# The 12-bit upper halves: from a VectorE bit shift to a ScalarE copy that rounds

## The chip, the cores and the metric

The kernel runs on one core of one Trainium2 chip. The metric is the device time of one execution in microseconds (us). The engines are written as in the profile: PE (TensorE matmul) and PEld (its weight loads), DVE (VectorE), ACT (ScalarE), POOL (GpSimd) and SP (SyncE, which issues the DMAs).

## The reference

The input is `x` (32 batches, 64 channels, 1024 positions) and a condition of 128 numbers for each batch. Two layers follow each other, and each has two parts.

The first part is a style-modulated stack of four 1-D convolutions (same, upsample, same, downsample, each with a kernel of 3), in which every batch has weights of its own:

```python
s = style @ mw.T + mb
weight = SCALE * w * s[:, None, :, None]
demod = lax.rsqrt(jnp.sum(weight * weight, axis=(2, 3)) + EPS)
weight = weight * demod[:, :, None, None]
```

The second part is a feed-forward block over tokens of 1024 numbers. In layer 0 it takes the 16 best of 64 experts, each a pair of rank-16 matrices (`h = x A`, gates, `o = (h * gate) B`). In layer 1 it is a product with int4 weights that have scales, zeros and a bias. All of it is to be computed at float32 precision.

## The kernel before, in words

**Tiling.** The 32 batches are 16 pairs `p`; a pair fills the 128 partitions with 2 x 64 channels for the convolutions. In the feed-forward part the partitions hold tokens or features. The convolution weights of a pair are first composed into one chain (`f`, L619, and `g`, L596, on PE; ACT copies `f` at L634 to L637, POOL adds at L642 to L652). `first` computes `c` (three matmuls, L768 and L773), ACT makes `yt` (L770), DVE adds (L774) and takes differences (L716), of which POOL takes more (L722, L730). `rest` makes the products `r` (L834, L843, L875) and `p` (L826), DVE adds (L865, L866, L883) and mends the edges with COPY_PREDICATED (L884). That is done for each half `h` of a pair.

**Exact products from short halves.** PE multiplies fast in the type float32r, which holds fewer bits than float32. So a number is cut into an upper and a lower half of 12 bits. `split` (L913 to L923) does this for the tokens: `high` (L149) clears the lower 12 bits by two shifts on DVE, PSUM to SBUF; DVE subtracts the result from PSUM, which gives the lower half `tl` (L919); ACT casts the upper half to `th` (L923). In layer 1 the cast of the second half of a pair is kept in a list (`held`) and put out later by `let_go` (L913). `turned_h` (L1079) does the same with transposed `h`, in tiles `ht`. `split_weights` does it for the weights `wa` and `wb`: shift on DVE (L149), subtraction on POOL (L374), cast on ACT (L375), and a DVE operation for the crossed term (L382). `scaled_low` (ACT, L927) scales the lower half and `crossed` (POOL, L935) makes `td`. The products are `h` and `o` (both L955) in layer 0 and `q` (L1204) in layer 1. The pairs 0 and 1 use plain float32 in layer 0.

**Stages.** The loop of layer 0 does the convolutions of the pairs beside the first product of the feed-forward block; its steady step takes 21.69 us (L826 at 201.37 and 223.06). A middle loop turns the gated `h` and makes the second product `o`. The loop of layer 1 does the convolutions of a pair beside `q` of the pair before.

**Order.** Work is put out in an order written by hand (lists like `beside`, and `yield` inside `layer0` and `layer1`, which lets the other work in). A scheduler then orders each engine's instructions; `tc.issue_after(x)` tells it to place an instruction behind `x`. PSUM banks come from three pools: `cps` with 3 banks (`c`, `r` and `ht`), `mps` with 1, and `fps` with 4 (`f`, `q`, and layer 1's second `r`). A new tile in a pool waits for the last reader of the tile that held its bank.

**Weights of layer 1's evacuation.** In `layer1` three pieces `q` (c = 0, 1, 2) of 342 columns are scaled by DVE into `sc` (L1228), added to `o` by POOL (L1230), and a scalar term is added by DVE (L1226). A copy of one element on POOL (`turn`, L1215) marks when the scales of the next pair may be loaded.

Of the kernel before, what the change touches and what calls it, by code (L numbers as in the profile page):

```python
# [8 lines left out]
F32 = mybir.dt.float32  # L9
I32 = mybir.dt.int32  # L10
F32R = mybir.dt.float32r
AF = mybir.ActivationFunctionType
ALU = mybir.AluOpType
AX = mybir.AxisListType

P = 128
# [9 lines left out]
H = 512  # L26
# [10 lines left out]
NB = 9  # L37
CHUNKS = ((0, 18), (18, 41), (41, 64))
AW = E + E * R
BITS = 12  # L40
RADIX = float(1 << BITS)


YD, YO, YE = HQ, 3 * HQ, 4 * HQ + 1
# [19 lines left out]
def adaln_ffn_kernel(ctx: ExitStack, tc: tile.TileContext, t, out: bass.AP):  # L64
    nc = tc.nc
# [4 lines left out]
    wk = ctx.enter_context(tc.tile_pool(name="wk", bufs=2))  # L70
# [8 lines left out]
    def cpst(name):  # L79
        return cps.tile([P, H], F32, tag="cps", name=name)  # L80
# [4 lines left out]
    def fpst(name):  # L85
        return fps.tile([P, H], F32, tag="fps", name=name)
# [51 lines left out]
    def tokens(tag, name, dt=F32R):  # L138

        return tok.tile([P, NC, P], dt, tag=tag, name=name, bufs=1 if tag == "td" else 2)  # L140

    def block(k, shape, dt, name):

        return wts.tile(shape, dt, tag=f"w{k}", name=name)

    def high(src, name):

        v = wk.tile([P, H], I32, tag="hi", name=name, bufs=3)[:, : src.shape[1]]
        nc.vector.tensor_scalar(  # L149
            v, src.bitcast(I32), BITS, BITS, ALU.logical_shift_right, ALU.logical_shift_left  # L150
        )
        return v.bitcast(F32)

    done, tbl, outers, uppers = {}, {}, {}, {}
    WHOLE = (0, 1)

    def nine(i, p):
# [209 lines left out]
    def split_weights(raw, w, ks, into, name, crossed=True):  # L367

        for k in ks:
            ws = block(k, [P, 3, w], F32R, f"{name}{k}")  # L370
            for c in range(0, w, H):
                cs = slice(c, min(c + H, w))
                h = high(raw[k][:, cs], f"{name}h{k}_{c}")
                nc.gpsimd.tensor_tensor(ws[:, 1, cs], raw[k][:, cs], h, ALU.subtract)  # L374
                nc.scalar.copy(ws[:, 0, cs], h)  # L375
            into[k] = ws
            if crossed:
                crossed_weights(into, k)

    def crossed_weights(into, k):  # L380
        ws = into[k]
        nc.vector.scalar_tensor_tensor(  # L382
            ws[:, 2], ws[:, 1], -RADIX, ws[:, 0], ALU.mult, ALU.add
        )
# [395 lines left out]
    def rest(i, n, y, f):  # L780
# [4 lines left out]
        p, h = n // 2, n % 2  # L785
        whole = i == 0 and p in WHOLE
        key = f"x{i}_{p}"
        if h == 0:
            th = tokens("th", f"th{key}", F32 if whole else F32R)
            toks[key] = [th] if whole else [th, tokens("tl", f"tl{key}")]  # L790
        hs = halves[h]
        th = toks[key][0][:, :, hs]
# [7 lines left out]
        if whole:  # L800
            yb, yo = y
            ps = cpst(f"r{i}_{n}")
            for j in range(4):
                for k in range(4):
                    v = (yo, yb)[(j + k) % 2]
                    o = j // 2 + k // 2 + (j % 2) * (k % 2)
# [7 lines left out]
            c = tbl[i, p][:, h, 1].unsqueeze(1).to_broadcast([P, 2 * 4, C])  # L814
# [3 lines left out]
        d = y[:, YD:YO].rearrange("p (a b) -> p a b", a=2)  # L818
# [13 lines left out]
        ps = cpst(f"r{i}_{n}_0")  # L832
# [39 lines left out]
        ps = (fpst if i == 1 and p > 0 else cpst)(f"r{i}_{n}_1")  # L872
        for j in range(4):
            q, k = j % 2, j // 2
# [6 lines left out]
            )  # L881

        nc.vector.tensor_tensor(ps, ps, both[:, :H], ALU.add)  # L883
        nc.vector.copy_predicated(  # L884
            ps.rearrange("p (j c) -> p j c", j=4)[:, 0::3],
            ident[:, 0 : P : P - 1].bitcast(I32).unsqueeze(2).to_broadcast([P, 2, P]),
            re[:, p % 2, h].unsqueeze(1).to_broadcast([P, 2, P]),
        )
        split(ps, shape, th, toks[key][1][:, :, hs], f"h{i}_{p}_{h}", i == 1 and h == 1 and p > 0)
        if i == 0 and h == 1:  # L890
            scaled_low(toks[key][1])

# [13 lines left out]

    held = []

    def let_go():

        while held:
            with tc.issue_after(done["fw"].ins):
                nc.scalar.copy(*held.pop())  # L913

    def split(ps, shape, hi, lo, name, hold=False):

        uppers[name] = high(ps, name)
        h = shape(uppers[name])
        done["lo"] = nc.vector.tensor_tensor(lo, shape(ps), h, ALU.subtract)  # L919
        if hold:  # L920
            held.append((hi, h))
        else:
            nc.scalar.copy(hi, h)  # L923

    def scaled_low(v):
        v = v.rearrange("p a b -> p (a b)")
        nc.scalar.activation(v, v, AF.Copy, scale=RADIX)  # L927

    toks = {}
# [10 lines left out]
    def at(k):  # L940

        return k ^ 1
# [22 lines left out]
    def layer0(p, ws):  # L965
# [5 lines left out]
        def joined(col, w, qd):  # L971
            dst = hs[:, col : col + w]
            if whole:
                nc.scalar.copy(dst, qd[0])
                return
            nc.scalar.activation(dst, qd[0], AF.Copy, scale=1.0 + 1.0 / RADIX)
            nc.vector.scalar_tensor_tensor(dst, qd[1], -1.0 / RADIX, dst, ALU.mult, ALU.add)

# [91 lines left out]
    def turned_h(p, hg):  # L1070
        whole = p in WHOLE
        key = f"h{p}"
        th = tokens("th", f"th{key}", F32 if whole else F32R)
        toks[key] = [th] if whole else [th, tokens("tl", f"tl{key}")]
        for g in range(2):
            ps = cpst(f"ht{p}_{g}")
            for c in range(4):
                k = 4 * g + c
                nc.tensor.transpose(  # L1079
                    ps[:, c * P : (c + 1) * P], hg[:, k * P : (k + 1) * P], ident  # L1080
                )
            ks = slice(4 * g, 4 * g + 4)

            def d(v):
                return v[:, ks].rearrange("p a b -> p (a b)")

            if whole:
                nc.scalar.copy(d(th), ps)
            else:
                split(ps, lambda v: v, d(th), d(toks[key][1]), f"hh{p}_{g}")  # L1090
        if not whole:
            scaled_low(toks[key][1])

# [14 lines left out]
    def layer0b(p, ws):  # L1108
# [10 lines left out]
        def joined(c, qd):  # L1119
            cs = slice(c * H, (c + 1) * H)  # L1120
            v = xres[:, cs]
            if not whole:
                nc.vector.scalar_tensor_tensor(v, qd[1], -SCALING / RADIX, v, ALU.mult, ALU.add)  # L1123
            nc.vector.scalar_tensor_tensor(  # L1124
                x4[:, c * P : (c + 1) * P],
                qd[0].rearrange("p (j f) -> p j f", f=4),
                SCALING if whole else SCALING * (1.0 + 1.0 / RADIX),
                v.rearrange("p (j f) -> p j f", f=4),
# [65 lines left out]
    def layer1(p, wq, aux):  # L1194


        o = residual.pop(p)
        for c in range(3):
            if c == 0:
                load_x1(p + 1)  # L1200
            ps = fpst(f"q{p}_{c}")[:, :QC]
            for j, half in enumerate(toks[f"x1_{p}"]):
                for k in range(NC):
                    nc.tensor.matmul(  # L1204
                        ps,
                        half[:, k],
                        wq[at(k)][:, c * QC : (c + 1) * QC],
                        start=(k == 0 and j == 0),
                        stop=(k == NC - 1 and j == 1),
                    )  # L1210
                if j == 0:
                    if c == 1 and p + 1 < NP:

                        turn = tiny.tile([P, 1], F32, tag="turn", name=f"turn{p}")
                        v = nc.gpsimd.tensor_copy(turn, uppers[f"h1_{p + 1}_0"][:, :1])  # L1215
                        with tc.issue_after(v.ins):
                            with_bias(p + 1, aux)
                    yield
            a = 2 if c == 0 else 0
            cs = slice(c * QC + a - 2, (c + 1) * QC - 2)  # L1220
            if c == 0:
                nrs = tiny.tile([P, 1], F32, tag="nrs", name=f"nrs{p}")
                nc.vector.tensor_scalar_mul(nrs, ps[:, 0:1], -1.0)
            if c == (0 if p == NP - 1 else 2):
                with tc.issue_after(done["lo"].ins):
                    nc.vector.scalar_tensor_tensor(o, aux[:, 1], nrs, o, ALU.mult, ALU.add)  # L1226
            s = wk.tile([P, QC], F32, tag="yt", name=f"sc{p}_{c}", bufs=2)[:, : QC - a]
            nc.vector.tensor_tensor(s, ps[:, a:], aux[:, 0, cs], ALU.mult)  # L1228
            eng = nc.vector if p == NP - 1 and c == 2 else nc.gpsimd
            eng.tensor_tensor(o[:, cs], o[:, cs], s, ALU.add)  # L1230
            if p == NP - 1:
                nc.sync.dma_start(out[p][:, cs], o[:, cs])
            yield
        if p < NP - 1:
            nc.sync.dma_start(out[p], o)

# [5 lines left out]
    xin, ys, gs, fw = {}, {}, {}, {}  # L1242
# [234 lines left out]
    for k in range(NP, 2 * NP):  # L1477
        begin(k + 2)
        tables_of(k + 3)
        outer_of(k + 2)  # L1480
        main = layer1(k - NP, *second)
        next(main)
        for fs in (
            (),
            ((later, k + 1, 0),),
            ((conv, k + 2, 0),),
            ((later, k + 1, 1),),
            ((weights, k + 2), (let_go,)),
        ):
            for f, *v in fs:  # L1490
                f(*v)
            next(main)
        conv(k + 2, 1)
        compose(k + 3)
        run(main)
        if k == NP:
            set_ends = ends(1, LAST, NP, block(7, [P, 3 * AW], F32, "room3"))
        elif k < NP + 8:
            next(set_ends, None)
# [44 lines left out]
```

## Time and profile before

| | us |
|---|---|
| median of 3 runs | 893.91 (893.53 to 894.51) |
| span of the profiled execution | 893.1 |
| what the median has beyond that span | 0.8 |
| mean granted TensorE clock of the profiled execution | 0.998 |

A profiled execution gives the time from its first to its last instruction; the run's time has a little around it, which is taken as the difference to the median. The page lists the busy time of each engine; a group of instructions has the line, the engine, the operation, what it writes and reads, how many there are, busy us and mean ns, and what ended the idle time before them. Overlapping instructions of one engine are seen in the timeline with starts closer than their lengths.

### The profile page before, as it was taken

The numbers are of one execution on the slowest core, as the hardware profiler recorded it, in microseconds if no ns is written. First come the engines' busy times: TensorE is split into PE (matmuls) and PEld (weight loads), VectorE is DVE, ScalarE is ACT, GpSimd is POOL, SyncE is SP. The second block draws the span as 40 slices with busy tenths as digits, with TensorE's granted clock in tenths as the row PEclk, the third lists the DMA queues.
The fourth block names the chain that finished last, engine by engine and source line by source line (L and its number), as shares of the span: only waits on it lengthen the run. The fifth ranks groups of instructions, "written<-read, shape, count | busy, mean of one in ns | idle before, by whom it ended". The sixth has DMA issues, their size and how long they took to land.

```text
span 893.1 us, 14916 instructions
## 1 busy us (share of the span) xinstructions
PE 866.1 (97%) x5033; PEld 775.1 (87%) x5033; DVE 723.2 (81%) x1460; ACT 352.4 (39%) x817; POOL 531.1 (59%) x745
## 2 busy tenths in 40 slices
PE   6989999999999999999999999999999999999997
PEld 4876888999999999994688888888899999999997
DVE  4475898888888888778986765669999999999996
ACT  6444544444444444333332221247333433343340
POOL 7235654666666666556572222343787888888884
PEclk9999999999999999999999999999999999999999
DMA  8632222222232222345475666555543334334321
GB/s 240 155 73 54 54 69 62 88 89 80 79 91 83 81 79 71 106 178 149 139 232 193 201 193 197 189 192 167 164 117 111 98 100 143 114 90 139 122 66 71
DMA packets 49739, 109.81 MB, mean 123 GB/s; under 512 B 13700, under 2 KB 22400, under 8 KB 49664
## 3 DMA queue, kind: packets, MB, share of 16 engines
q1 hardware_dynamic: 48704, 107.88, 39.5%
q10 hardware_dynamic: 960, 0.99, 0.5%
q8 instruction: 40, 0.66, 0.3%
q14 instruction: 35, 0.29, 0.1%
HBM read 70.97 MB, written 37.88 MB: 122 GB/s over the span
## 4 chain that ended last, share of the span: by engine, by line
PE 42%; DVE 7%; POOL 2%; issue 2%; ACT 0%; DVEq 0%; POOLq 0%; ACTq 0%
PE o L955 16%; PE q L1204 11%; PE f L619 3%; PE r L875 3%; PE c L773 2%; PE r L834 1%; PE r L843 1%; PE c L768 1%; PE ht L1079 1%; PE g L596 1%; DVE cv L716 1%; DVE x L1124 1%; PE p L826 1%; DVE rt L866 1%; DVE r L884 0%
## 5 line engine op out<-in xcount | busy, mean ns | idle before, releaser
L716 DVE TENSOR_TENSOR cv<-cv 128x257 f32<-128x257 f32 x120 | 105.8, 913 | 1.3 <-ACT cv L758 0.9
L730 POOL TENSOR_TENSOR cv<-cv 128x256 f32<-128x256 f32 x120 | 77.7, 647 | 29.8 <-DVE cv L716 25.1
L722 POOL TENSOR_TENSOR cv<-cv 128x128 f32<-128x128 f32 x100 | 39.0, 411 | 67.5 <-PE r L843 48.3
L1204 PE MATMUL q<-wq,thx 128*128 128x342 f32 x384 | 73.0, 332 | 2.1 <-ACT thx L913 2.1
L955 PE MATMUL h<-wa,tdx 128*128 128x352 f32 (+1 forms) x336 | 72.2, 351 | 0.2 <-DVE wa L382 0.2
L1204 PE MATMUL q<-wq,tlx 128*128 128x342 f32 x384 | 72.3, 330 | 0.0
L619 PE MATMUL f<-gs,iw 128*128 128x128 f32 (+1 forms) x384 | 68.2, 327 | 0.1
L619 PEld LDWEIGHTS f<-gs,iw 128*128 128x128 f32 x384 | 61.8, 190 | 5.9 <-issue 0.5
L955 PE MATMUL h<-wa,thx 128*128 128x352 f32 (+1 forms) x336 | 64.7, 333 | 0.0
L1204 PEld LDWEIGHTS q<-wq,thx 128*128 128x128 f32 x384 | 60.3, 189 | 4.1 <-ACT thx L913 3.2
L770 ACT ACTIVATE yt<-c,be,al 128x257 f32<-128x257 f32 x56 | 31.7, 567 | 80.4 <-PE c L768 77.3
L875 PE MATMUL r<-cv 128*128 128x128 f32 x480 | 63.4, 274 | 0.0
L1204 PEld LDWEIGHTS q<-wq,tlx 128*128 128x128 f32 x384 | 61.9, 189 | 0.8
L955 PE MATMUL h<-wa,tlx 128*128 128x352 f32 (+1 forms) x336 | 62.4, 327 | 0.0
L955 PE MATMUL o<-wb,thh 128*128 128x512 f32 x224 | 60.4, 402 | 1.5 <-ACT wb L375 1.5
L935 POOL TENSOR_TENSOR tdx<-thx,tlx 128x1024 fp32r<-128x1024 f32 x14 | 34.7, 2479 | 44.5 <-ACT tlx L927 36.2
L955 PEld LDWEIGHTS h<-wa,tdx 128*128 128x128 f32 x336 | 56.9, 188 | 2.4 <-DVE wa L382 0.5
L1123 DVE SCALAR_TENSOR_TENSOR cv<-o,cv 128x512 f32<-128x512 f32 x26 | 18.0, 692 | 50.2 <-PE o L955 50.2
L955 PE MATMUL o<-wb,tlh 128*128 128x512 f32 x224 | 58.4, 397 | 0.0
L875 PEld LDWEIGHTS r<-cv 128*128 128x128 f32 x480 | 58.4, 191 | 0.0
L634 ACT COPY cv<-f 128x256 f32<-128x256 f32 x64 | 24.0, 375 | 83.9 <-PE f L619 46.3
L642 POOL TENSOR_TENSOR cv<-cv 128x256 f32<-128x256 f32 x60 | 50.0, 833 | 11.4 <-ACT cv L637 11.4
(313 smaller groups left out, 2274.6 us busy)
## 6 DMA issues: line engine op xcount, KB each, us to landing
cv<-in_x_dram SPq DMA_DIRECT2D x60, 256.0 KB
cv<-x1e SPq DMA_DIRECT2D x64, 192.5 KB
x1e<-dd SPq DMA_DIRECT2D x16, 514.0 KB
hgd<-hs SPq DMA_DIRECT2D x16, 512.0 KB
hg<-hgd SPq DMA_DIRECT2D x16, 512.0 KB
x1d<-x SPq DMA_DIRECT2D x16, 512.0 KB
xb<-x1d SPq DMA_DIRECT2D x16, 512.0 KB
out_dram<-o SPq DMA_DIRECT2D x15, 512.0 KB
```

Source lines behind the costliest of these rows:

```text
L619: done["f"] = nc.tensor.matmul(pv[:, n : n + 2 - k], iw[:, e].rearrange("p a b -> p (a b)"), v, start=(m == 0), stop=(m == len(steps) - 1) ...
L634: nc.scalar.copy(f8[:, 0::2], pv[:, :, h])
L642: nc.gpsimd.tensor_tensor(f[:, 4 * P : 6 * P].rearrange("p (a b) -> p a b", b=P), v[:, :, 0], v[:, :, 1], ALU.add,)
L716: nc.vector.tensor_tensor(d[:, k], yo[:, k : k + HQ], yb, ALU.subtract)
L722: nc.gpsimd.tensor_tensor(y[:, YB + k * P : YB + (k + 1) * P], y[:, 2 * k : 2 * k + 2 * P - 1 : 2], y[:, 1 : 2 * P : 2], ALU.subtract,)
L730: nc.gpsimd.tensor_tensor(e[:, :, k], d[:, :, 2 * k : 2 * k + HQ - 2 : 2], d[:, :, 1 : HQ - 1 : 2], ALU.subtract,)
L770: nc.scalar.activation(yt, mid, AF.Identity, bias=be0[:, n : n + 1], scale=a)
L875: done["r"] = nc.tensor.matmul(ps[:, j * P : (j + 1) * P], y[:, YE + (2 * q + k) * P : YE + (2 * q + k + 1) * P], w(q + 2 * k), start=True ...
L935: done["td"] = nc.gpsimd.tensor_tensor(*(v.rearrange("p a b -> p (a b)") for v in (td, *toks[key])), ALU.subtract)
L955: nc.tensor.matmul(banks[l == 2], toks[key][l][:, order(k)], w[:, cols], start=(k == first and l != 1), stop=(k == last and l in (2, min(n ...
L1123: nc.vector.scalar_tensor_tensor(v, qd[1], -SCALING / RADIX, v, ALU.mult, ALU.add)
L1204: nc.tensor.matmul(ps, half[:, k], wq[at(k)][:, c * QC : (c + 1) * QC], start=(k == 0 and j == 0), stop=(k == NC - 1 and j == 1),)
```

## The change

`high` is gone. ACT writes the upper half from PSUM straight into a float32r tile, which rounds it; DVE then subtracts what ACT wrote. For the weights ACT rounds the raw weights and POOL subtracts that. In layer 1 both subtractions of a pair (not ACT's casts) are held: that of the first half goes behind the scaling of `q` at c = 0, that of the second behind the scalar term at c = 2, and both of these are placed behind COPY_PREDICATED (`done["edges"]`). The evacuation of c = 0 is put out one `yield` later. `turn` reads the float32r half.

```diff
-    def high(src, name):
-
-        v = wk.tile([P, H], I32, tag="hi", name=name, bufs=3)[:, : src.shape[1]]
-        nc.vector.tensor_scalar(
-            v, src.bitcast(I32), BITS, BITS, ALU.logical_shift_right, ALU.logical_shift_left
-        )
-        return v.bitcast(F32)
...
             for c in range(0, w, H):
                 cs = slice(c, min(c + H, w))
-                h = high(raw[k][:, cs], f"{name}h{k}_{c}")
-                nc.gpsimd.tensor_tensor(ws[:, 1, cs], raw[k][:, cs], h, ALU.subtract)
-                nc.scalar.copy(ws[:, 0, cs], h)
+                nc.scalar.copy(ws[:, 0, cs], raw[k][:, cs])
+                nc.gpsimd.tensor_tensor(
+                    ws[:, 1, cs], raw[k][:, cs], ws[:, 0, cs].bitcast(F32), ALU.subtract
+                )
...
-        nc.vector.copy_predicated(
+        done["edges"] = nc.vector.copy_predicated(
...
-        split(ps, shape, th, toks[key][1][:, :, hs], f"h{i}_{p}_{h}", i == 1 and h == 1 and p > 0)
+        split(shape(ps), th, toks[key][1][:, :, hs], i == 1 and p > 0)
...
-    def let_go():
+    def let_go(behind):
 
         while held:
-            with tc.issue_after(done["fw"].ins):
-                nc.scalar.copy(*held.pop())
-
-    def split(ps, shape, hi, lo, name, hold=False):
-
-        uppers[name] = high(ps, name)
-        h = shape(uppers[name])
-        done["lo"] = nc.vector.tensor_tensor(lo, shape(ps), h, ALU.subtract)
-        if hold:
-            held.append((hi, h))
-        else:
-            nc.scalar.copy(hi, h)
+            with tc.issue_after(behind.ins):
+                nc.vector.tensor_tensor(*held.pop(), ALU.subtract)
+
+    def split(v, hi, lo, hold=False):
+
+        nc.scalar.copy(hi, v)
+        held.append((lo, v, hi.bitcast(F32)))
+        if not hold:
+            done["lo"] = nc.vector.tensor_tensor(*held.pop(), ALU.subtract)
...
-                        v = nc.gpsimd.tensor_copy(turn, uppers[f"h1_{p + 1}_0"][:, :1])
+                        first = toks[f"x1_{p + 1}"][0][:, 0, :1].bitcast(F32)
+                        v = nc.gpsimd.tensor_copy(turn, first)
...
+            if c == 0:
+                yield
...
-                with tc.issue_after(done["lo"].ins):
-                    nc.vector.scalar_tensor_tensor(o, aux[:, 1], nrs, o, ALU.mult, ALU.add)
+                with tc.issue_after(done["edges"].ins):
+                    v = nc.vector.scalar_tensor_tensor(o, aux[:, 1], nrs, o, ALU.mult, ALU.add)
+                let_go(v)
...
-            nc.vector.tensor_tensor(s, ps[:, a:], aux[:, 0, cs], ALU.mult)
+            with tc.issue_after(done["edges"].ins) if held else nullcontext():
+                v = nc.vector.tensor_tensor(s, ps[:, a:], aux[:, 0, cs], ALU.mult)
+            if c == 0:
+                let_go(v)
...
-            yield
+            if c > 0:
+                yield
...
-            ((weights, k + 2), (let_go,)),
+            ((weights, k + 2),),
```

More of the change, by code (lines that the diff above doesn't have):

```diff
@@ L39 @@
 AW = E + E * R
-BITS = 12
-RADIX = float(1 << BITS)
+RADIX = float(1 << 12)
 YD, YO, YE = HQ, 3 * HQ, 4 * HQ + 1
@@ L144, in block @@
         return wts.tile(shape, dt, tag=f"w{k}", name=name)
-    def high(src, name):
-        v = wk.tile([P, H], I32, tag="hi", name=name, bufs=3)[:, : src.shape[1]]
-        nc.vector.tensor_scalar(
-            v, src.bitcast(I32), BITS, BITS, ALU.logical_shift_right, ALU.logical_shift_left
-        )
-        return v.bitcast(F32)
-    done, tbl, outers, uppers = {}, {}, {}, {}
+    done, tbl, outers = {}, {}, {}
     WHOLE = (0, 1)
@@ L1089, in turned_h @@
             else:
-                split(ps, lambda v: v, d(th), d(toks[key][1]), f"hh{p}_{g}")
+                split(ps, d(th), d(toks[key][1]))
         if not whole:
```

## The prediction

> **What bounds the kernel now.** I read the page first, for the shares of the engines.
>
> ```profile
> PE 866.1 (97%) x5033; PEld 775.1 (87%) x5033; DVE 723.2 (81%) x1460; ACT 352.4 (39%) x817; POOL 531.1 (59%) x745
> ```
>
> TensorE (PE) is busy 866.1 of 893.1 us: about 27 us are idle in all, and whatever frees VectorE (DVE) can gain only there. The busy times of single stretches say where these are (columns: stretch, length, then busy us of PE, weight load, DVE, ACT, POOL, the granted clock, DMA):
>
> ```profile
> 42.00:64.00 22.00, 19.47 (x110) 15.49 (x109) 17.59 (x35) 11.44 (x25) 9.85 (x11) 1.00 0.31 75
> 201.00:223.00 22.00, 22.00 (x140) 20.91 (x138) 18.80 (x44) 10.04 (x23) 13.54 (x20) 1.00 0.28 80
> 603.00:625.00 22.00, 20.68 (x117) 17.70 (x116) 21.06 (x47) 15.58 (x33) 7.03 (x37) 1.00 0.56 166
> 759.00:781.00 22.00, 22.00 (x145) 21.24 (x144) 21.16 (x38) 8.09 (x22) 18.44 (x26) 1.00 0.38 115
> ```
>
> In the steady steps of layer 0 (201 to 223) and of layer 1 (759 to 781) PE has no gap; it has some at the start, at the change of layers and at the end. The waits of PE name them (waited in all, times, longest):
>
> ```profile
> PE c L773 <- DVE rt L866: 2.2, 3, 1.1
> PE q L1204 <- ACT thx L913: 2.1, 3, 0.9
> PE r L834 <- POOL cv L648: 1.9, 2, 1.1
> PE c L773 <- DVE tlx L919: 1.8, 2, 1.3
> PE o L955 <- ACT wb L375: 1.5, 2, 0.9
> PE ve L535 <- DVE room L521: 1.2, 1, 1.2
> ```
>
> **What is removed and added.** From the groups by line (busy us, mean ns, idle before):
>
> ```profile
> L149 DVE TENSOR_SCALAR h<-r 128x512 int32<-128x512 int32 x60 | 41.2, 686 | 1.5
> L149 DVE TENSOR_SCALAR hh<-ht 128x512 int32<-128x512 int32 x28 | 18.9, 681 | 0.0
> L149 DVE TENSOR_SCALAR wbh<-cv 128x512 int32<-128x512 int32 x16 | 14.3, 929 | 2.8 <-POOL wb L374 2.8
> L923 ACT CAST thx<-h 128x512 fp32r<-128x512 f32 x45 | 27.8, 618 | 45.0 <-DVE h L149 44.2
> L1088 ACT COPY thh<-ht 128x512 f32<-128x512 f32 x4 | 2.0, 598 | 0.0
> ```
>
> Gone from DVE are these shifts and 24 shifts of `wa` (11.1 + 2.0 us): 41.2 + 18.9 + 14.3 + 13.1 = 87.5 us of its 723.2. Every ACT copy stays, only its source changes, from SBUF to PSUM or the raw weights. A PSUM source is shown by L1088, 598 ns against 618: 60 + 28 copies at 0.02 less are 1.8 us of an engine that is 39% busy, so I count nothing. PE's work is the same. The subtraction L919 keeps its 0.68 us, but it now waits for ACT instead of for DVE's own shift.
>
> The Trainium skill's "Perfetto Trace Analysis" (Optimizing Scalar/DVE Operations) says that work may go from a saturated DVE to ScalarE. Layer 1's window has DVE at 21.16 of 22 us, which would invite that, yet PE is at 22.00 there. By the rule, read as a gain for what DVE sheds, layer 1's 32 shifts at 0.686 would count, an estimated 22 us. The sum goes by the row: nothing there.
>
> **Gains, idle spot by idle spot** (times are starts of the waiting matmul in PE's timeline).
>
> 1. 46.09 (0.84), 52.01 (1.20), 59.84 (0.49), all for DVE's small operations on `room`: 2.53. In front of them DVE's timeline has two `wah` shifts of together 1.94 us at 42.69 and one of 0.18 at 48.15. Their removal covers it: I take 2.4 (0 to 2.5).
> 2. 82.16 (0.78, POOL's sum): no shift lies before it, 0.
> 3. 113.07 (1.12, L866): the three `kept` shifts, 1.96 us, lie right before L865 and L866; all 1.12 goes, and the 0.17 at 119.46. At 125.00 (0.57) the subtraction must now wait for an ACT copy of 0.62, nearly the shift's 0.68: 0.3. At 135.34 (1.15, POOL) DVE and POOL are both a little earlier: 0.6. Together 2.2 (1.1 to 3.0).
> 4. 430.87 and 432.28 (0.63 + 0.91): `wb` was cut behind DVE's queue (means of 929 ns, and 2.17 us for the three shifts at 429.41). ACT now takes it from the raw weights without DVE: 1.5 (0.7 to 1.5).
> 5. 496.43 and 580.24 (0.53 + 0.30): DVE's queue only, 0.3 (0 to 0.8).
> 6. 620.32 (1.26, `tlx`): COPY_PREDICATED ends at 618.08, the copy would end at 618.75 and the subtraction at 619.45, against 620.18: 0.7. 632.19: 0.2 of 0.30. 642.12 (0.74, `thx`), which came behind shift and held copy: 0.7. Together 1.6 (0.7 to 2.3).
> 7. 684.81 and 703.49 (0.32 + 0.72, L866): a DVE that is one shift behind, 0.8 (0 to 1.0).
> 8. 868.01 and 880.82 (0.41 + 0.92, `thx`): the copy starts behind COPY_PREDICATED, 0.7 earlier: 0.4 + 0.7 = 1.1 (0.5 to 1.3).
>
> Sum: 2.4 + 2.2 + 1.5 + 0.3 + 1.6 + 0.8 + 1.1 = 9.9 us, between 3.0 and 12.4.
>
> **A loss in layer 0's steady steps.** `c` and `r` share three PSUM banks. In the built order of the changed kernel the third `c` matmul (L773) of the second half of each step takes the bank that the step's `r` leaves with its subtraction; before, it took the one that ACT's `yt` left. That is so in nine steps (the odd `c` from 13 to 29) and begins in that of 11. One such step, before, DVE:
>
> ```profile
> 213.73 0.42 DVE L884 COPY_PREDICATED r<-ident,re 128x256 f32<-128x256 int32 x1
> ...
> 214.33 0.68 DVE L149 TENSOR_SCALAR h<-r 128x512 int32<-128x512 int32 x1
> ...
> 215.32 0.67 DVE L919 TENSOR_TENSOR tlx<-r,h 128x512 fp32r<-128x512 f32 x1
> ```
>
> and PE:
>
> ```profile
> 214.36 0.70 PE L773 MATMUL c<-cv,c 128*128 128x256 f32 x2
> ```
>
> DVE is some 0.37 earlier by then (the first half's shift is gone, but its subtraction waits for ACT), so COPY_PREDICATED ends at 214.15 - 0.37 = 213.78, `thx` on ACT at 214.45, `tlx` at 215.17, and the matmul that was free to go at 214.36 starts at about 215.25: 0.9 us of idle PE per step. ACT's `yt` also moves behind `thx` here, to about 215.5; that costs PE nothing, since DVE's next reader of it waits for the same `c`. The time is not won back: at the next step's L865 DVE waits 2.57 us for PE, so the whole step moves. The trace of before has this very dependency once in layer 0:
>
> ```profile
> 125.00 0.67 PE L773 MATMUL c<-cv,c 128*128 128x256 f32 x2 [0.57 <-DVE tlx L919]
> ```
>
> It cost 0.57 there. I take 0.7, between that row and the walk's 0.9: 9 x 0.7 = 6.3, and 0.2 for the step of 11: 6.5 us. Bounds: 0 (at 366.29 the last step had the same dependency with no idle, but there no differences L684 and L687, 0.98 and 0.94 us, stood before COPY_PREDICATED) and 1.2 per step (no DVE lead), 11.
>
> **What is moved and costs nothing.** In the middle stage the subtraction of `hh` waits for ACT as well; PE is without a gap from 447 to 580 but for one spot, and the tokens are used one step later. In layer 1 both subtractions of a step are held until behind the evacuations of `q` at c = 0 and c = 2; behind them on DVE stand `rt` and the `yt` sums, which are released as much earlier by the missing shifts (2 x 0.686 per step of 17.06). POOL's `turn` copy (0.19 us) waits for ACT instead of DVE: `thx` ends about when the shift did. SP's queue is passed by nothing.
>
> **Sum.** 9.9 - 6.5 = 3.4 us. The profiled span is 893.1, 0.8 below the median of 893.91 for what lies around it, and that stays: 893.9 - 3.4 = 890.5.
>
> **Rivals.**
> - *No new PSUM wait* (DVE's lead grows, or PE arrives later with other work): 893.9 - 9.9 = 884.0. For it: the bank is held for less long, copy and subtraction being 1.4 us against 1.84 from 214.15 to 215.99. Against: a lead of 0.37 does not cover 0.9.
> - *Layer 1's f sums come late, slower.* `thx` of the second half now stands before ACT's six copies of `f` (L634 to L637), whose POOL sums free the product `p` (L826). Before, the first L652 ended at 800.84 and L826 started at 802.54: 1.70 us of cover. Now the copies begin when COPY_PREDICATED (797.80, with a lead of 0.5: 797.3) and the 0.62 of `thx` are over, at 797.91 instead of 796.86: the sums come 1.05 later. POOL is busy 18.44 of 22 us there, and L652 took 1.45 instead of 0.51 when DVE contended; a second such stretch of 0.94 makes 1.99, and a `turn` of 0.19 in POOL's queue 2.2. From 1.70 on it decides: (2.2 - 1.7) x 14 steps = 7.0, so 890.5 + 7.0 = 897.5.
> - *The idle only moves on.* The next producer is late where the first was early, and half of the gains stay: 893.9 - 5.0 + 6.5 = 895.4.
>
> **How the numbers follow.** The forecast 0.47 (its own range 888 to 894), no new wait 0.25, late sums 0.16, moved idle 0.12. A measurement of this kernel tells about 0.2%, 1.8 us: faster is below 892.1, slower above 895.7. The forecast case gives 0.28 faster, 0.14 same and 0.05 slower, the second 0.25 faster, the third 0.01 same and 0.15 slower, the fourth 0.01 faster, 0.05 same and 0.06 slower: 0.54, 0.20, 0.26. The range 884 to 898 leaves out half of the second case and the far end of the third.
>
> **What would show it.** In the profile after: no L149 shift of `r` or `ht`; DVE near 636 us; no waits at 46, 52, 113 and 431; a wait of `c` for DVE `tlx` nine or ten times, about 0.7 each, with layer 0's step going from 21.69 to about 22.4 us; layer 1's step still at 17.06. The prediction is wrong if that wait is absent or over 1.2, if PE waits for POOL's L652 or ACT's `yt` in layer 1, or if DVE's subtraction shows more than 0.8 us.

## The result: 25.6 us slower, and the profile after

| | before | changed |
|---|---|---|
| median of 4 runs each, same chip | 894.08 (893.53 to 894.51) | 919.66 (918.5 to 920.71) |
| span of the profiled execution | 893.1 | 916.9 |

The ratio is 1.0281 (95% interval 1.0269 to 1.0294). The prediction, 890.5 and "faster" as the likeliest, is wrong, and the time lies far beyond its range.

The first line of the page after says that the removal itself went as forecast: DVE does 78.6 us less. What grew is above all PE's idle time, from 27 to 46.7 us; PE's busy time grew by 4.1 us, from 866.1 to 870.2.

```profile
PE 870.2 (95%) x5033; PEld 777.6 (85%) x5033; DVE 644.6 (70%) x1332; ACT 340.2 (37%) x817; POOL 512.6 (56%) x745
```

The waits of PE after (waited in all, times, longest) say for whom. Two of these lines were forecast, the first, at 0.7 a time, and the `thx` one, as a leftover; the others are new or have grown.

```profile
PE c L765 <- DVE tlx L912: 9.8, 11, 1.4
PE o L944 <- DVE x L1113: 6.8, 1, 6.8
...
PE c L765 <- DVE rt L858: 5.9, 4, 3.9
PE h L944 <- ACT hs L963: 3.0, 1, 3.0
...
PE q L1193 <- ACT thx L909: 1.3, 1, 1.3
PE r L826 <- ACT yt L762: 0.8, 5, 0.2
```

Line numbers after are some 8 to 11 lower than before: L765 is `c` (L773 before), L944 the products `h` and `o` (L955), L1113 `x` (L1124), L858 `rt` (L866), L762 `yt` (L770), L826 `r` (L834 before, not the `p` that had this number).

The busy time in stretches about the same work as the prediction's (stretch, length, then busy us of PE, weight load, DVE, ACT, POOL, the granted clock, DMA), with one about the hole in the middle stage:

```profile
42.00:64.00 22.00, 22.00 (x134) 18.61 (x133) 10.51 (x26) 8.09 (x17) 1.23 (x2) 1.00 0.34 80
202.00:224.60 22.60, 21.80 (x139) 20.66 (x138) 16.98 (x42) 9.60 (x23) 12.48 (x19) 1.00 0.25 77
436.00:459.00 23.00, 15.63 (x70) 12.56 (x71) 10.54 (x18) 6.91 (x17) 4.12 (x16) 0.85 0.67 204
780.00:802.00 22.00, 21.86 (x143) 20.86 (x143) 19.56 (x35) 6.70 (x18) 17.52 (x25) 1.00 0.39 123
```

At the start PE has no gap left (19.47 of 22 before). In layer 0's step 0.8 us are idle. At 436 to 459 no engine is even half busy but PE: that is a chain of waits, not a lack of engine time. Beside PE only the DMA engines are busy for more than half of it (0.67), and for all of 436 to 443 (share 1.02), when the transfers behind a late `x` come together. The hole also costs more than its length. In the 3.8 us behind it (453.4 to 457.2) PE works without a pause, but the granted clock is 0.53, and eight matmuls of `o` take 3.74 us, against 2.06 just before the hole:

```profile
444.54 2.06 PE L944 MATMUL o<-wb,tdh 128*128 128x512 f32 x8 [0.38 <-DVE cv L302]
453.37 3.74 PE L944 MATMUL o<-wb,tdh 128*128 128x512 f32 x8 [6.78 <-DVE x L1113]
```

Over the whole execution the clock is 0.993, before 0.998.

To see where the time came in, I took the starts of the same matmuls in PE's timelines of both kernels; the difference is how late the changed kernel is by then.

| matmul | before | changed | later by | added in the stretch | forecast for it |
|---|---|---|---|---|---|
| a `c` at the end of the start-up | 147.97 | 145.62 | -2.35 | -2.35 | -4.6 |
| the `p` at the end of layer 0's steps | 374.98 | 382.19 | 7.21 | +9.56 | +6.5 |
| the first `c` of layer 1 | 592.06 | 605.79 | 13.73 | +6.52 | -1.8 |
| a `p` early in layer 1 | 644.72 | 663.23 | 18.51 | +4.78 | -1.6 |
| a `p` near the end of layer 1 | 853.74 | 876.85 | 23.11 | +4.60 | -0.8 |
| end of the span | 893.1 | 916.9 | 23.8 | +0.7 | -1.1 |

The forecasts add to -3.4, the measured to +23.8. Only layer 0's loss was foreseen, and it was foreseen too small. Each of the others was read in the trace.

**Layer 0.** DVE, ACT and PE in a step (start, us):

```profile
214.44 0.42 DVE L876 COPY_PREDICATED r<-ident,re 128x256 f32<-128x256 int32 x1
...
215.57 0.69 DVE L912 TENSOR_TENSOR tlx<-r,thx 128x512 fp32r<-128x512 f32 x1 [0.45 <-ACT thx L909]
```

```profile
214.95 0.59 ACT L909 CAST thx<-r 128x512 fp32r<-128x512 f32 x1 [4.74 <-DVE r L876]
```

```profile
216.40 0.67 PE L765 MATMUL c<-cv,c 128*128 128x256 f32 x2 [0.80 <-DVE tlx L912]
```

It is the forecast chain: COPY_PREDICATED, ACT's copy, the subtraction, the bank, `c`. It cost 0.80 to 0.81 in nine steps and 1.39 in that of 11 (the eleventh wait of that row, 1.15 at 627.06, is in layer 1).

**The weight `wa7` (107 us).** ACT, in the changed kernel:

```profile
101.30 0.56 ACT L750 ACTIVATE cv<-c,be,al 128x256 f32<-128x256 f32 x1
105.54 1.14 ACT L364 CAST wa<-kept 128x512 fp32r<-128x512 f32 x2 [3.68 <-POOL wa L365]
106.58 0.81 ACT L963 COPY hs<-h 128x352 f32<-128x352 f32 x2
```

The code holds the cutting of the last weight block back with `tc.issue_after(done["gates"].ins)`, an anchor on DVE. It held DVE's shift, and ACT's copy came behind that shift by data. Now the first operation is ACT's copy, and an anchor on DVE does not order ACT's queue. The copies stand ahead of the copies of `hs`, and wait 3.68 us for POOL, which is subtracting the block before (`wa`, 102.04 to 105.5). Before, these copies of `hs` began at 103.65 and the casts came behind them:

```profile
103.65 0.81 ACT L974 COPY hs<-h 128x352 f32<-128x352 f32 x2
...
110.41 1.73 ACT L375 CAST wa<-wah 128x512 fp32r<-128x512 f32 x3 [1.32 <-DVE wah L149]
```

In the changed kernel PE's `h` waits 2.99.

**The weights `wb` (407 to 453 us).** DVE, in the changed kernel:

```profile
425.18 2.27 DVE L374 SCALAR_TENSOR_TENSOR wb<-wb 128x1024 fp32r<-128x1024 f32 x1 [1.16 <-POOL wb L365]
427.38 1.05 DVE L1113 SCALAR_TENSOR_TENSOR x<-o,xres 128x512 f32<-128x512 f32 x1
428.62 2.27 DVE L374 SCALAR_TENSOR_TENSOR wb<-wb 128x1024 fp32r<-128x1024 f32 x1 [0.20 <-POOL wb L365]
432.05 1.23 DVE L374 SCALAR_TENSOR_TENSOR wb<-wb 128x1024 fp32r<-128x1024 f32 x1 [1.16 <-POOL wb L365]
433.19 1.04 DVE L1113 SCALAR_TENSOR_TENSOR x<-o,xres 128x512 f32<-128x512 f32 x1
...
443.32 1.07 DVE L1113 SCALAR_TENSOR_TENSOR x<-o,xres 128x512 f32<-128x512 f32 x1 [6.56 <-DMA xres<-in_x_dram]
```

Before, the first residual sums `x` stood on DVE behind four of the eight crossed terms of `wb`:

```profile
412.01 1.23 DVE L382 SCALAR_TENSOR_TENSOR wb<-wb 128x1024 fp32r<-128x1024 f32 x1 [2.39 <-POOL wb L374]
413.15 1.96 DVE L1124 SCALAR_TENSOR_TENSOR x<-o,xres 128x512 f32<-128x512 f32 x2
```

Now six stand in front, each waiting for POOL's subtractions (one stretch of 24.1 us from 407.92), and `x` starts at 427.38. On it depend, on SP, the stores of `x` and `dd`, and behind them in SP's queue stands the load of the next residual:

```profile
435.63 0.59 SPq L1161 DMA_DIRECT2D x1e<-dd  x1
436.27 0.62 SPq L1094 DMA_DIRECT2D xres<-in_x_dram  x1
```

Before, that load was issued at 417.53. DVE waits 6.56 us for it and then 5.69 for a load of weights (`in_cw`), and PE waits 6.78 at 453.37 for the bank that the last of these `x` frees.

**The start of layer 1.** `dd` and `rt` share one buffer, and DVE's `rt` now waits for the store of the last `dd`:

```profile
639.95 3.38 DVE L1157 TENSOR_TENSOR dd<-x 128x510 f32<-128x510 f32 x1
...
647.92 0.42 DVE L857 TENSOR_TENSOR rt<-r,tbl 128x256 f32<-128x256 f32 x1 [4.08 <-DMA x1e<-dd]
```

PE's `c` waits 3.89 for it at 649.22.

**Layer 1's steps.** ACT, before and in the changed kernel:

```profile
789.42 0.57 ACT L770 ACTIVATE yt<-c,be,al 128x257 f32<-128x257 f32 x1 [2.95 <-PE c L768]
790.92 0.62 ACT L923 CAST thx<-h 128x512 fp32r<-128x512 f32 x1 [0.94 <-DVE h L149]
```

```profile
812.20 0.59 ACT L909 CAST thx<-r 128x512 fp32r<-128x512 f32 x1 [4.16 <-DVE r L876]
812.69 0.57 ACT L762 ACTIVATE yt<-c,be,al 128x257 f32<-128x257 f32 x1
```

`yt` could have gone at about 810.8, when PE was done with `c`. It now stands behind the copy, which waits for COPY_PREDICATED. It frees the bank of the next `r` late: `r` starts 0.54 behind `p`, where it started 0.23 behind it before (791.34 and 791.57).

```profile
812.77 0.39 PE L818 MATMUL p<-cv 128*128 128x128 f32 x2
813.31 0.74 PE L826 MATMUL r<-cv 128*128 128x128 f32 x4 [0.15 <-ACT yt L762]
```

A step takes 17.48 instead of 17.06. The Trainium skill's "Perfetto Trace Analysis" (Tensor Engine Instruction) states that ACT, DVE and GpSimd are strictly first in, first out; ACT's rows here, `hs` at 106.58 and `x` at 427.38 all agree with it.

### The profile page after: what moved, and what is told of

Read it like the earlier page. It is cut to its first block, busy times and chain, and to the rows that moved or that the text cites. A ratio compares the mean times of both kernels' runs of the same rounds, so it can differ in the third digit from the quotient of the medians.

```text
span 916.9 us, 14756 instructions
## 1 busy us (share of the span) xinstructions
PE 870.2 (95%) x5033; PEld 777.6 (85%) x5033; DVE 644.6 (70%) x1332; ACT 340.2 (37%) x817; POOL 512.6 (56%) x745
## 4 chain that ended last, share of the span: by engine, by line
PE 45%; DVE 28%; issue 8%; POOL 7%; ACT 6%; DMA 4%; SPq 0%; ACTq 0%; DVEq 0%; POOLq 0%
PE o L944 13%; PE h L944 12%; DVE cv L708 5%; PE f L611 4%; DVE r L875 3%; PE q L1193 3%; DVE rt L858 3%; POOL wb L365 2%; DVE cv L766 2%; DVE r L876 2%; PE c L765 2%; PE r L826 2%; ACT thx L909 2%; PE r L799 1%; PE r L867 1%
## 5 line engine op out<-in xcount | busy, mean ns | idle before, releaser
L909 ACT CAST thx<-r 128x512 fp32r<-128x512 f32 x60 | 35.1, 585 | 256.9 <-DVE r L876 155.3
L722 POOL TENSOR_TENSOR cv<-cv 128x256 f32<-128x256 f32 x120 | 76.4, 636 | 53.4 <-DVE cv L708 26.3
L708 DVE TENSOR_TENSOR cv<-cv 128x257 f32<-128x257 f32 x120 | 92.7, 804 | 2.0 <-ACT cv L750 1.9
L944 PE MATMUL h<-wa,tdx 128*128 128x352 f32 (+1 forms) x336 | 71.3, 350 | 0.0
L766 DVE SCALAR_TENSOR_TENSOR cv<-c,al,yt 128x257 f32<-128x257 f32 x112 | 50.8, 477 | 24.7 <-ACT yt L762 24.3
L944 PE MATMUL h<-wa,thx 128*128 128x352 f32 (+1 forms) x336 | 64.8, 334 | 3.0 <-ACT hs L963 3.0
L944 PE MATMUL o<-wb,tdh 128*128 128x512 f32 x224 | 56.7, 402 | 7.3 <-DVE x L1113 6.8
L634 POOL TENSOR_TENSOR cv<-cv 128x256 f32<-128x256 f32 x60 | 44.5, 742 | 32.6 <-ACT cv L629 30.5
L1226 POOL TENSOR_TENSOR o<-o,sc 128x342 f32<-128x342 f32 (+1 forms) x47 | 46.1, 982 | 29.5 <-DVE sc L1222 27.3
L944 PE MATMUL h<-wa,tlx 128*128 128x352 f32 (+1 forms) x336 | 62.3, 326 | 0.0
L944 PE MATMUL o<-wb,thh 128*128 128x512 f32 x224 | 59.2, 399 | 0.0
L944 PEld LDWEIGHTS h<-wa,tdx 128*128 128x128 f32 x336 | 56.7, 188 | 1.9
```

The source lines that it names most:

```text
L634: nc.gpsimd.tensor_tensor(f[:, 4 * P : 6 * P].rearrange("p (a b) -> p a b", b=P), v[:, :, 0], v[:, :, 1], ALU.add,)
L708: nc.vector.tensor_tensor(d[:, k], yo[:, k : k + HQ], yb, ALU.subtract)
L722: nc.gpsimd.tensor_tensor(e[:, :, k], d[:, :, 2 * k : 2 * k + HQ - 2 : 2], d[:, :, 1 : HQ - 1 : 2], ALU.subtract,)
L766: nc.vector.scalar_tensor_tensor(d, ps, a, yt[:, :w_], ALU.mult, ALU.add)
L909: nc.scalar.copy(hi, v)
L944: nc.tensor.matmul(banks[l == 2], toks[key][l][:, order(k)], w[:, cols], start=(k == first and l != 1), stop=(k == last and l in (2, min(n ...
```

## The experiments

My theory was then: the loss is no lack of engine time. It is made of separate waits, and each comes from an in-order queue or a bank rotation that the change re-ordered. The rivals: the longer chain of DVE, ACT, DVE is dear by itself, wherever it stands; or early idle only moves on, and one part makes the whole loss. First I took each part of the change alone. Ratios are to the kernel before on the same chip, with their 95% interval. Most differences are near one per cent or below; a run is called slower or faster where its interval leaves out 1.

**Layer 0's `r` alone.** The kernel before, with this in `rest`:

```diff
+        if i == 0:
+            nc.scalar.copy(th, shape(ps))
+            nc.vector.tensor_tensor(lo, shape(ps), th.bitcast(F32), ALU.subtract)
+        else:
             split(ps, shape, th, ...)
```

> The kernel before, with ACT's rounded copy and DVE's difference for layer 0's r alone; weights, ht and layer 1 as before. Theory (each part of the change brings a wait of its own, through the order and the PSUM banks it leads to): the odd c matmuls from 11 to 29 take the bank that the subtraction of r frees, as in the changed kernel, so nine waits of PE c for DVE tlx of 0.8 us and one of about 1.4, layer 0's step 22.5 instead of 21.7, and no other new wait: 894.1 + 9 = about 903. Rival (the losses hang together, one late transfer or one engine that runs late through the whole kernel): the part alone costs little, under 3 us.

Measured 903.45 (ratio 1.0087, 1.0066 to 1.0107). PE's waits:

```profile
PE c L773 <- DVE tlx L931: 8.7, 10, 1.4
```

The 8.7 are 1.4 once and 0.81 nine times, against a loss of 8.0: this one wait is as large as the whole loss of the part.

**The weights alone.**

```diff
-                h = high(raw[k][:, cs], f"{name}h{k}_{c}")
-                nc.gpsimd.tensor_tensor(ws[:, 1, cs], raw[k][:, cs], h, ALU.subtract)
-                nc.scalar.copy(ws[:, 0, cs], h)
+                nc.scalar.copy(ws[:, 0, cs], raw[k][:, cs])
+                nc.gpsimd.tensor_tensor(
+                    ws[:, 1, cs], raw[k][:, cs], ws[:, 0, cs].bitcast(F32), ALU.subtract
+                )
```

> The kernel before, with the new split_weights alone (wa and wb). Theory: the early waits of ue, ve, g and of c for rt at 113 go, 3 to 5 us gained before 150 us; at 400 to 460 us DVE's order puts the first residual sum x behind six crossed-term operations of wb instead of four, and POOL, which does the 16 subtractions one after the other, holds them: 2 to 7 us lost there; in all 892 to 898. Rival: only the gain, 888 to 890.

Measured 901.08 (1.0068, 1.005 to 1.0086). The early gains are there, and then two waits eat them:

```profile
PE o L956 <- DVE x L1125: 6.3, 1, 6.3
...
PE h L956 <- ACT hs L975: 2.8, 1, 2.8
```

**The turned `h` alone** (`split` in `turned_h` replaced by ACT's copy and DVE's subtraction).

> The kernel before, with ACT's rounded copy and DVE's difference for the turned h (ht) alone. Theory: DVE's order around 400 to 460 us moves with it, the first x behind five crossed-term operations and the second behind nine, so x, its transfers and the next load of the residual come late: 2 to 7 us slower, all of it before 460 us; from there to 600 us PE stays without gaps. Rival: the middle stage is bound by PE and the part is free, 893 to 894.5.

Measured 905.91 (1.0124, 1.0103 to 1.0146), the dearest of the four, where the prediction had counted nothing.

```profile
PE o L960 <- DVE x L1129: 6.5, 1, 6.5
...
PE ht L1084 <- DVE tlh L928: 3.4, 1, 3.4
```

The weights are cut here as before, and still DVE's order of `x` against the crossed terms of `wb` changed: the second `x` starts at 429.89, behind the last of the eight crossed terms (eight, not the nine of the expectation). So the scheduler moved instructions that the edit does not touch; why it places them so is not shown.

**Layer 1's part alone** (the held subtractions, the anchors and `turn` as in the change, all else as before).

> The kernel before, with everything of the change that concerns layer 1 (copy from PSUM, held subtractions, the moved yield, turn). Theory: yt of layer 1 comes behind thx on ACT and frees its PSUM bank late for r, 0.4 us per pair of batches in steps of 17.06, 4 to 5 us over layer 1, and 0 to 5 at its start around 645 us: 898 to 904. Rival: layer 1 stays bound by PE, and what was lost there in the changed kernel came from the late start: within 1 us of 894.

Measured 905.19 (1.0114, 1.0093 to 1.0135), the later steps 17.5 us.

```profile
PE c L773 <- DVE rt L866: 7.5, 4, 4.1
...
PE r L834 <- ACT yt L770: 0.8, 5, 0.2
```

So all four parts lose: 8.0 + 5.6 + 10.4 + 9.7 = 33.7 us, against 25.6 for all together. The sum is larger mainly since the parts of the weights and of `h` each make the same late `x` (6.3 and 6.5), which the changed kernel waits for once (6.8). That the whole loss is one part's is refuted.

Next, each part alone with its cause taken away. If the copy and the subtraction are dear by themselves, the loss stays.

**Layer 0 with another bank** for the `r` of the second half.

```diff
-        ps = (fpst if i == 1 and p > 0 else cpst)(f"r{i}_{n}_1")
+        ps = (fpst if (i == 1 and p > 0) or (i == 0 and h == 1 and p > 1) else cpst)(f"r{i}_{n}_1")
```

> As the kernel with layer 0's part alone, but the second half's r of a step gets its PSUM bank from the pool of four (fps) instead of the pool of three that it shares with c. ACT's copy, DVE's wait for it and all instructions stay. Theory (the bank is what costs): the third c matmul now takes the bank that rt frees 2 us earlier, its nine waits for tlx of 0.8 us go, layer 0's step is 21.7 again, and the time is within 1.5 us of the kernel before. Rival (the later subtraction costs by itself, through tl, tdx or the later yt): the step stays at about 22.5 and the time at +8.

Measured 899.35 (1.0043, 1.0026 to 1.0059): half of the loss is back. The wait for `tlx` in the steady steps is gone, and a step takes 22.19, where it took 22.56 without the other bank and 21.69 in the kernel before. PE and POOL show what is late next:

```profile
PE p L826 <- POOL cv L652: 3.6, 9, 0.7
```

```profile
219.31 1.13 POOL L1011 TENSOR_TENSOR hs<-hs,ga 128x368 f32<-128x368 f32 x1 [1.15 <-DVE hs L985]
```

POOL's gate waits for DVE's `hs`; the `f` sums stand behind it in POOL's queue, and `p` waits 0.36 in each step. A second limit lay 0.4 us behind the first. That chain was not repaired.

**The weights with their two orders back.** ACT's copies of the last block are held behind ACT's Exp of the gates (an anchor on ACT), and the crossed terms 4 to 7 of `wb` behind the first `x`.

```diff
-            nc.scalar.activation(ga, s0, AF.Exp, bias=su)
+            done["exp"] = nc.scalar.activation(ga, s0, AF.Exp, bias=su)
...
-            with tc.issue_after(done["gates"].ins):
+            with tc.issue_after(done["exp"].ins):
                 split_weights(araw, AW, (7,), wa, "wa", False)
...
-                crossed_weights(into, k)
+                late = name == "wb" and k > 3
+                with tc.issue_after(done["x0"].ins) if late else nullcontext():
+                    crossed_weights(into, k)
```

> As the kernel with the weights' part alone, but two orders are put back by hand: ACT's copies of the kept weights stand behind ACT's exponential of the gates (before, DVE's shift, which is gone, was held behind the gates), and DVE's crossed terms of wb 4 to 7 stand behind the first residual sum x. Theory (the lost hold and DVE's order cost): the wait of h for ACT hs at 108 (2.8 us) and that of o for DVE x at 447 (6.3 us) go, the gains at 46 to 60 stay: 3 to 5 us faster than the kernel before. Rival (POOL's run of 16 subtractions is what holds the middle stage, in whatever order): still 5 us or more slower than before.

Measured 890.32 (0.9941, 0.9921 to 0.9961): faster than before by 4.7 us. Both waits are gone from PE's list, those of the start stay gone. The two orders, about 10 us (5.6 lost without them, 4.7 won with them), were the whole loss of this part, and hid its gain.

**The turned `h` with the order of `wb` back** (the last edit of the one above).

> As the kernel with the part of ht alone, but DVE's crossed terms of wb 4 to 7 stand behind the first residual sum x. Theory: tlh at 431 (3.4 us) and x at 450 (6.5 us) are waited for only because they stand behind nine crossed terms on DVE; with the order put back both go and the time is within 2 us of the kernel before. Rival (the subtraction that waits for ACT holds the turned h): 431 stays, 3 us or more slower.

Measured 898.24 (1.004, 1.0022 to 1.0058). The wait of 3.4 is gone; one of 4.1 is left:

```profile
PE o L962 <- DVE x L1131: 4.1, 1, 4.1
```

So the order of `wb` explains most of it (a loss of 3.2 is left of 10.4), but this one anchor is not enough here.

**Layer 1 with the first copy behind `yt`.** The first half's copy is anchored to `yt`, and the next scales to POOL's sum of `q` at c = 0 instead of to `turn`.

```diff
+            with tc.issue_after(done["yt"].ins):
+                nc.scalar.copy(hi, v)
+            nc.vector.tensor_tensor(lo, v, hi.bitcast(F32), ALU.subtract)
...
-                        v = nc.gpsimd.tensor_copy(turn, first)
-                        with tc.issue_after(v.ins):
+                        with tc.issue_after(done["sc"].ins):
                             with_bias(p + 1, aux)
```

> As the kernel with layer 1's part alone, but the first half's copy thx stands behind yt on ACT (its subtraction follows it), and the POOL copy that marks the next scales is replaced by POOL's own sum of q_0. Theory (yt behind thx frees the bank of r late): layer 1's step is 17.06 again instead of 17.5, 4 us of the 9.7 come back; the 4.1 us at the start of layer 1, which have another cause (rt waits for a transfer out of its own buffer), stay: 898 to 900 where the kernel before takes 894. Rival (ACT's f copies or POOL's sums set the step): the step stays at 17.5.

Measured 899.18 (1.0046, 1.0026 to 1.0067), the step 17.07 again. ACT's rows have changed places:

```profile
759.25 0.57 ACT L770 ACTIVATE yt<-c,be,al 128x257 f32<-128x257 f32 x1 [2.95 <-PE c L768]
759.71 0.58 ACT L920 CAST thx<-r 128x512 fp32r<-128x512 f32 x1
```

What is left, 4.2 us, is at the start of layer 1 (`rt`, 2.42 at 642.05) and at the end. The edit also lets the first subtraction follow its copy at once and takes `turn` from POOL's queue; the run does not separate these from the order of `yt`, for which the rows above speak.

**The repairs in the changed kernel.** First only the weights' two orders, then all four.

> The changed kernel with the two orders of the weights' part put back by hand (ACT's copies of the kept weights behind the exponential, DVE's crossed terms of wb 4 to 7 behind the first x). Theory (the losses of the parts are separate and these two stand for 3.0 us at 107 and 7.8 us at 436 to 453): 8 to 11 us faster than the changed kernel, 908 to 912, with the waits for tlx in layer 0 and layer 1's step of 17.5 as they were. Rival (in the whole change another producer takes their place): under 4 us come back.

Measured 907.27 (1.0136, 1.0117 to 1.0155): the loss is halved, by two orders alone.

> The changed kernel with all four repairs: the weights' orders, layer 0's second r in the other PSUM pool, layer 1's first thx behind yt. Theory: 919.7 less 10 (orders), 4 (bank), 4 (yt) and 1.5 (start of layer 1) is about 900, so it stays slower than the kernel before by some 5 us, since POOL's sums in layer 0 and the transfer at the start of layer 1 remain. Rival (the repairs free DVE's whole relief, and with 87 us less work on DVE it is faster than before): under 892.

Measured 895.03 (1.0007, 0.9993 to 1.0022, ten runs): the same as before. With every shift gone and the same copies and subtractions (only `turn` is replaced as well), order and one bank make about 25 of the 25.6 us. That the longer chain of DVE, ACT, DVE is dear wherever it stands is refuted with it. PE's list still has waits that no repair reached, `p` for POOL's sums (ten times, 4.0 in all) and `rt` (2.8 at most); that they alone keep it from a gain is likely, but was not tested. The reverse, the kernel before with its shifts but with these orders spoiled, was not run either.

**Weights and `h` with their orders back, `r` as before.**

> The kernel before with the weights' part and the part of ht, both with the orders put back; layer 0's r and layer 1 as before. Theory (these two parts lie where PE had waits for DVE or ACT, and ht brings nothing there as PE is without gaps): 889 to 892, like the weights' part alone, and faster than both kernels. Rival (ht's wait for x at 441, 4.1 us with ht alone, remains): 893 to 895.

Measured 888.34 (0.9932, 0.9915 to 0.9949): faster than both kernels. Its page:

```profile
PE 863.1 (97%) x5033; PEld 774.2 (87%) x5033; DVE 688.0 (78%) x1392; ACT 346.9 (39%) x817; POOL 534.7 (60%) x745
```

Here DVE sheds 35 us and PE's idle time falls by 4 (the other 3 us of the span are PE's busy time, of which the clock, 1.000 against 0.998, explains under 2); the changed kernel's DVE sheds 79 and PE is idle for 20 more.

**Layer 1's part, with `dd` in a buffer of its own** for the last pair.

```diff
-        dd = wk.tile([P, 4 * HQ], F32, tag="rt", name=f"dd{p}", bufs=1)
+        own = dict(tag="w4", bufs=3) if p == NP - 1 else dict(tag="rt", bufs=1)
+        dd = wk.tile([P, 4 * HQ], F32, name=f"dd{p}", **own)
```

> As the kernel with layer 1's part alone, but the last pair's dd has a buffer of its own (a tile of the tag w4), not that of rt. Theory (in the new order of DVE the first rt of layer 1 that follows dd must wait for the transfer of dd to memory, as they share one buffer): the wait of c for rt at 634.6, 4.1 us, goes, and the time is 3 to 4 us under the 905 of the part alone; the step of 17.5 stays. Rival (the late dd comes from POOL's long sum beside it, 3.4 us, and the wait is for DVE): 2 us or more of the wait stay.

Measured 902.45 (1.0096, 1.0081 to 1.0111), hardly less than without, and the intervals overlap. The wait of 4.1 is gone, but another took most of its place:

```profile
PE p L826 <- POOL cv L652: 2.9, 1, 2.9
```

**All but layer 0's part, with the orders, `yt` and `dd`.**

> Weights and ht with their orders put back, layer 1's part with the first thx behind yt and the own buffer of dd, layer 0's r with DVE's shift as before. Theory: layer 1's step is that of the kernel before, the waits of q for thx at the end (0.4 and 0.9 us) and the transfer's wait are gone: 887 to 890, beside 888.3 for weights and ht alone. Rival (layer 1's part still loses at its start or end): 890 to 893.

Measured 891.19 (0.9966, 0.9954 to 0.9979): faster than before, yet slower than without layer 1's part (888.34; the two intervals just fail to meet). With its known waits repaired, that part seems still to cost, by `p` (2.7 at 640.14) and `rt` (1.4 and 1.1) at the start of layer 1. Which order of PE's own work would avoid that stays open; it was not tried.

## Why the prediction was wrong, point by point

- **Gain 1: right.** The waits at 46, 52 and 59 are gone, as is that at 113 of gain 3. To 148 us, the 2.35 won and the new 2.99 make 5.3, against 4.6 forecast; that is a net figure, with another new wait of 1.21 at 32.64 (`rows` for DVE's `room`) in it.
- **Gains 2 and 3: the failed step is what was not looked at between them.** I listed the idle spots of before and asked which of them would go; I did not ask which new one would come. The wait at 107 was in the built order, ACT's copies of `kept` ahead of `hs`.
- **Gain 4, "ACT now takes it from the raw weights without DVE": right in itself, and the wrong question.** The 0.63 and 0.91 at 431 are gone. But without the shifts the scheduler put two more crossed terms in front of `x` in DVE's queue. The step priced instructions as if every other one kept its place; together with the part of `h`, it cost +6.5 instead of -1.8 in the stretch.
- **Gains 6 and 8: overrun.** The 1.26 at 620 became 1.15 at 627, and behind it came the 3.9 of `rt`. At the end `thx` 1.3 and `tlx` 0.5 are left where 0.2 was expected: the subtraction behind ACT's copy is new there. Gain 7 is not seen: `c` still waits 0.65 and 1.17 for `rt` in layer 1's first steps.
- **The loss in layer 0: the mechanism was right, the sizes off.** The term 0.7 measured 0.81; the walk of 0.9 and the row of 0.57 bound it. The term of the step of 11, 0.2, measured 1.39. Sum 8.7 for 6.5. The Trainium skill's "Perfetto Trace Analysis" (Optimization Strategy) says that the same gap repeated on the engine that should be busy can mean too little PSUM for the next tile. The row agrees, 0.81 in nine steps, and another bank ended it; yet it gave back only half the time, since POOL's sums were 0.36 late behind it.
- **"What is moved and costs nothing": this failed, and with gain 4 it is most of the error.** The stretches of the middle stage and of layer 1 make 21.9 of the 27.2 us between the forecast -3.4 and the measured +23.8. The middle stage was called gapless and so safe; `h` alone cost 10.4. Layer 1's steps were said to stay at 17.06, as both subtractions are held; but it is ACT's copy, which is not held, that blocks ACT's queue. "SP's queue is passed by nothing" was true of what is put out, and false of time: the load of the residual stood behind stores of a late `x`.
- **The rivals.** The first did not happen. The second looked at the right place, a copy ahead in ACT's queue in layer 1, but at the wrong victim: the `f` copies behind the second half's copy had cover, `yt` behind the first half's had none, and the price was 0.42 a step, not 0.5 x 14 through POOL. The third, that idle moves on, came true twice (POOL's sums behind the bank in layer 0, `p` behind `dd`) but not as a mean of half the gains.
- **DVE at 636:** measured 644.6, though every removal is there. The 87.5 was taken whole from 723.2, and the two are counted differently: instructions that follow each other on DVE overlap (a shift of 0.68 starts at 214.33, the next instruction at 214.93), a group's sum counts the overlap twice, the page once. DVE's groups add to 797.5 before and 700.9 after, a fall of 96.6; the page's figure falls by 78.6. Changes of length nearly cancel: L679 (L687 before) took 16.6 us more, L708 (L716) 13.1 and L676 (L684) 4.4 less.
- The prediction called itself wrong if PE waits for ACT's `yt` in layer 1, or if the wait in layer 0 is over 1.2; both were seen.

## What to carry to other kernels

An instruction that is removed takes with it what it did for order: an anchor that held it, the place that others had behind it in its queue, the reader that freed a bank. So price a removal by walking the built order of every queue, and for each instruction that moved to another engine ask what stands behind it there while it waits; an anchor must be on the engine whose queue it is to order. Here, with PE busy 97% of the time, 79 us less of DVE was worth nothing by itself, and a wait of half a microsecond in a repeated step outweighed it.

## What the runs showed of the hardware

ACT's 128x512 cast to float32r took 585 ns in the mean from PSUM, against 618 from SBUF: the price of the replacement was as good as forecast, and its place was not.

```profile
L909 ACT CAST thx<-r 128x512 fp32r<-128x512 f32 x60 | 35.1, 585 | 256.9 <-DVE r L876 155.3
```

DVE's `dd` of 128x510, 0.68 us in 12 of its 16 cases, took 3.38 at 639.95, while POOL ran this sum from 639.44 on:

```profile
639.44 3.33 POOL L1176 TENSOR_TENSOR o<-xb,aux 128x1024 f32<-128x1024 f32 x1
```

It ended 0.56 after POOL's sum did. The Trainium skill's "SBUF — State Buffer" (SBUF: two separate sides) states that a DVE operation with two SBUF inputs and a GpSimd operation that reads SBUF shut each other out for a whole instruction; the row agrees, with 3.38 us for 0.68, and with `dd` in its own buffer it ran at 628.89, clear of POOL's sum at 635.41, and took 0.68 again. So a re-ordered queue also changes how long its instructions take.
